# Keys and values of a cross attention layer by one level of Strassen's scheme, on a kernel in float32

## The chip, the core and the metric

The kernel runs on one core of a Trainium2 chip. TensorE multiplies matrices into PSUM; VectorE (DVE), ScalarE (ACT) and GpSimd (POOL) work elementwise on SBUF, the first two also on PSUM; SyncE (SP) issues most of the DMAs, in order. Each engine works through its own queue of instructions in program order and waits on semaphores for the others. The metric is the device time of one execution in microseconds, as a median over runs.

## The reference, cut to what matters

A perceiver of two layers over x (16 batches of 64 queries, 512 channels) and a context (16 batches of 1601 rows, 512 channels). Everything is float32. The change is in the second layer, L1, and at its border to the first:

```python
x = x + L0_xattn(...); x = x + L0_attn(...); x = x + L0_ffn(...)      # experts, top 2 of 8 and 2 shared
# L1 cross attention: D = 512, H = 16 heads of HD = 32
q = split_heads(layernorm(x) @ Wq + bq)          # 64 queries a batch
k = split_heads(ctx @ Wk + bk)                   # 1601 keys a batch
v = split_heads(ctx @ Wv + bv)
scores = where(mask, -1e15, einsum('bhqd,bhkd->bhqk', q, k) / sqrt(32))
o = einsum('bhqk,bhkd->bhqd', softmax(scores), v)
x = x + o @ Wo + bo
# per row of x: differential attention over 32 half heads of 16, then a feed forward 512-2048-512 (relu)
x = x + L1_attn(layernorm(x), ...)
# feed forward with ternary weights and quantised activations, with a width 3 convolution along the queries
x = x + L1_ffn(layernorm(x), ...)
```

K and V of the context, 16 x 1601 x 512 x 512 multiplications each, are the largest matrix products of the layer.

## The kernel before, in words

x is held as eight tiles `g.x[t]` of 128 rows (two batches each), which stay in SBUF from the first line to the last. L0 ends in `l0_ffn`: experts write their results to a DRAM buffer `worked`, and a last loop gathers them by GpSimd's indirect DMAs and adds them to the tiles of x (L666). The weights Wk and Wv are loaded there already (`g.wk`, `g.wv`). Tiles come from pools; a tile with a tag and n buffers waits for the last reader of the n-th one before it. The PSUM tags are `mm` (4 banks), `tp` (2) and `acc` (2).

`l1_layer` is a loop over 16 batches b, and in each over four groups f of four heads (128 channels). The keys of a batch are cut into four tiles `KC` of 384, 384, 384 and 449.

- `load_ctx(b)` loads the transposed context, channels on the partitions, as four tiles `ctxT` and `ctxT_last`; it is called when f = 2 of the batch before is done.
- `project_k(b, f, n)` makes K transposed for one group f and one key tile: four accumulating matmuls whose moving tensor is the context tile (384 or 449 columns); ScalarE copies it to `kT` with the bias. In step (b, f) it is called for the group that comes next, for all four tiles.
- `project_v(b, half, n)` makes V with keys on the partitions, for 256 channels: per 128 keys four matmuls whose stationary tensor is the context and whose moving tensor is Wv, 256 columns; ScalarE copies it to `v`. Called in the even steps for f // 2.
- `scores` makes the scores of two banks at a time, and VectorE's `copy_predicated` (L832) writes the unmasked ones into `p`, which GpSimd has filled with -1e15 (L1192). Then per `p` a maximum on VectorE (L1202) and an exponential on ScalarE (L1203).
- `transpose_keys` (L182, L185) transposes the p of the step before, and `attend` (L842) multiplies it with v. So the softmax of a step is used one step later.
- `finish` scales the output by the reciprocal row sums: rs8 is transposed (L855), inverted on VectorE, and spread over the channels by eight pairs of matmuls with the constant `spread` (L861). For the second batch of a tile Wo, and the residual into `g.x[t]`, follow.
- `queries(t)` makes the queries of a tile of x, with Wq loaded in halves.
- `later(t)` is the rest of the layer for a tile that has its cross attention: a generator with a `yield` after each piece. Its large VectorE work is `products` (L895 multiplies, L896 sums, 16 rounds for q by k and 8 for the weights by v). It ends in `last(t)`, the ternary feed forward.

The order of the work is written out by hand: after the scores of a step, four rounds n = 0 to 3 follow, each with `project_k`, in round 0 also `attend`, in even steps `project_v`, and then `run(behind, quota)`, that lets so many pieces of `later` of the tile before run. `later(t)` begins at f = 0 of an even batch and runs out at the end of the odd one. In the first two batches `behind` is `ternary_weights`, which prepares the ternary weights. Before the loop, batch 0's context is loaded, K and V of its first groups are made, and the queries of tile 0.

`load_cols` and `load_rows` load weights in pieces of 512 KB from a pool of six buffers; `load_row` loads a bias row, spread over the partitions, once for the whole layer (x1_bo, a1_bo, a1_b2).

Of the kernel before, what the change touches and what calls it, by code (L numbers as in the profile page):

```python
# [2 lines left out]

# [7 lines left out]
F32 = mybir.dt.float32  # L11
# [426 lines left out]
def l0_ffn(g, d):  # L438
# [8 lines left out]
    with ExitStack() as es:  # L447
# [210 lines left out]
        for t in range(NT):  # L658
            for k in range(2):
# [8 lines left out]
                )  # L668


KC = [(0, 384), (384, 384), (768, 384), (1152, 449)]


def l1_layer(g, d, out):
# [5 lines left out]
    with ExitStack() as es:  # L680
# [3 lines left out]
        cpool = pool("x1_c", 3)  # L684
        kpool = pool("x1_k", 6)
        vpool = pool("x1_v", 15)
# [3 lines left out]
        spool = pool("x1_s", 1)  # L690
        apool = pool("a1_s", 1)
        prod = pool("a1_prod", 1)
        wpool = pool("l1_w", 6)

        x1bo = load_row(g, one, "x1_bo")
        a1bo, b2 = load_row(g, one, "a1_bo"), load_row(g, one, "a1_b2")
# [6 lines left out]
        spread = one.tile([NP, 2, NC, P], F32, tag="spread", name="spread")  # L703
        nc.gpsimd.memset(spread, 0.0)
        for j in range(2):
            for pl in range(2):
                nc.gpsimd.memset(spread[:, j, :, ds((2 * pl + j) * HDX, HDX)], 1.0)
            nc.gpsimd.affine_select(
                out=spread[:, j], in_=spread[:, j], compare_op=ALU.is_equal, fill=0.0,
                base=0, pattern=[[-2, NC], [-1, 2], [0, 2 * HDX]], channel_multiplier=1,  # L710
            )
# [37 lines left out]
        ctxs, kTs, vs = {}, {}, {}  # L749

        def load_ctx(b):
            for n, (k0, w) in enumerate(KC):
                tag = "ctxT" if n < 3 else "ctxT_last"
                t = cpool.tile([P, NC, w], F32, tag=tag, name=tag, bufs=None if n < 3 else 1)
                nc.sync.dma_start(
                    out=t, in_=g.ctx_T[b, :, k0 : k0 + w].rearrange("(c p) k -> p c k", p=P)
                )
                ctxs[b, n] = t

        def project_k(b, f, n):  # L760

            w = KC[n][1]
            ps = mm(g)
            mm_k(g, ps[:, :w], lambda c: wk[:, c, ts(f, P)], lambda c: ctxs[b, n][:, c, :])
            tag = "kT" if n < 3 else "kT_last"
            kT = kpool.tile([P, w], F32, tag=tag, name=tag, bufs=None if n < 3 else 2)
            nc.scalar.activation(kT, ps[:, :w], AF.Identity, bias=col(g, "x1_bk", f))  # L767
            kTs[b, f, n] = kT

        def project_v(b, half, n):  # L770

            k0, w = KC[n]
            for k in range((w + P - 1) // P):
                kw = min(P, w - k * P)
                ps = mm(g)
                mm_k(
                    g, ps[:kw, :256],
                    lambda c: ctxs[b, n][:, c, ds(k * P, kw)],
                    lambda c: wv[:, c, ts(half, 256)],
                )  # L780
                v = vpool.tile([P, 256], F32, tag="v", name="v")
                nc.scalar.copy(v[:kw], ps[:kw, :256])  # L782
                vs[b, half, k0 // P + k] = v[:kw]

        def queries(t):

            u = apool.tile([P, D], F32, tag="u2", name="u")
            ln_apply(g, u, g.x[t], ln_stats(g, small, [g.x[t]]), 0)
            yield
            uT = apool.tile([P, NC, P], F32, tag="u2T", name="uT")  # L790
            nc.scalar.copy(uT, transpose4(g, u))
            yield
# [5 lines left out]
            qT = spool.tile([P, NC, P], F32, tag="qT", name="qT", bufs=2)  # L798
# [37 lines left out]
        def attend(b, f, pTs, po):  # L836
# [3 lines left out]
            for k in reversed(range(len(KT))):  # L840
                for r in reversed(range(4)):
                    nc.tensor.matmul(  # L842
                        po[ts(r, HDX), ts(f, S)],
                        lhsT=vs[b, f // 2, k][:, ts(4 * (f % 2) + r, HDX)],
# [6 lines left out]
        def finish(b, po, rs8):  # L851
            t, hb = divmod(b, 2)

            pt = mm(g, tag="tp")
            nc.tensor.transpose(pt[:NP, :P], rs8, g.ident)  # L855
            rsT = small.tile([NP, P], F32, tag="rsT", name="rsT")
            nc.vector.reciprocal(rsT, pt[:NP, :P])
            pr = mm(g, tag="tp")
            for f in range(NC):
# [503 lines left out]
```

## Time and profile before

| what | value |
|---|---|
| median of 3 runs | 3542.52 us (3540.64 to 3544.93) |
| the profiled execution, by the device | 3548.19 us |
| its span, first to last instruction | 3546.4 us |
| mean granted clock of TensorE | 0.968 |
| L146 MATMUL, K, 384 columns | 1536, busy 555.2 us |
| L146 MATMUL, V, 256 columns, context tiles 0 to 2 | 2304, busy 523.7 us |
| L146 MATMUL, V, tile 3 | 1024, busy 226.2 us |
| L146 MATMUL, K, 449 columns | 512, busy 206.4 us |
| L832 COPY_PREDICATED, L1202 maximum, DVE | 270.4 and 226.5 us |
| L895 and L896, products, DVE | 156.5 and 155.8 us |
| L185 and L782, copies of pT and v, ACT | 230.7 and 152.4 us |
| L1192 memset of p, POOL | 185.7 us |

A group of instructions has a mean duration, but the records of TensorE overlap: the time between starts of neighbours is what a matmul costs in a stream. A float32 matmul leaves two records and two weight loads. The idle time of an engine before a group is put down to what released it last. The first 790 us are L0; the loop over batches starts at about 843 us, and two batches take between 321 and 326 us. The chain of work that ended last is followed on the page only through part of the span, TensorE 9% and DVE 6%, so the windows and the timeline carry more.

### The profile page before, as it was taken

The numbers are of one execution on the slowest core, as the hardware profiler recorded it, in microseconds if no ns is written. First come the engines' busy times: TensorE is split into PE (matmuls) and PEld (weight loads), VectorE is DVE, ScalarE is ACT, GpSimd is POOL, SyncE is SP. The second block draws the span as 40 slices with busy tenths as digits, with TensorE's granted clock in tenths as the row PEclk, the third lists the DMA queues.
The fourth block names the chain that finished last, engine by engine and source line by source line (L and its number), as shares of the span: only waits on it lengthen the run. The fifth ranks groups of instructions, "written<-read, shape, count | busy, mean of one in ns | idle before, by whom it ended". The sixth has DMA issues, their size and how long they took to land. (4 is left out here: it accounts for less than half of the span.)

```text
span 3546.4 us, 49781 instructions
## 1 busy us (share of the span) xinstructions
PE 3275.7 (92%) x21128; PEld 2194.3 (62%) x21128; DVE 1652.8 (47%) x2632; ACT 1140.0 (32%) x2220; POOL 377.5 (11%) x340
## 2 busy tenths in 40 slices
PE   6999999998999999999999999999999999999815
PEld 2444445685677666766767666667667676666514
DVE  2121223116525825653493458256534934581573
ACT  1111021112333434334333434343343334343402
POOL 0000003332101100010001001000100010010000
PEclk9999999999999999999999999999999999999957
DMA  9988413875611133113222321331132123213113
GB/s 361 313 288 304 140 36 107 283 254 174 196 50 50 40 107 103 57 43 123 95 65 74 111 75 40 107 103 57 44 124 97 61 74 111 75 41 107 63 36 122
DMA packets 267374, 418.03 MB, mean 118 GB/s; under 512 B 20736, under 2 KB 164224, under 8 KB 267152
## 3 DMA queue, kind: packets, MB, share of 16 engines
q1 hardware_dynamic: 254656, 370.28, 31.7%
q0 software_dynamic: 12496, 44.57, 3.6%
q8 instruction: 166, 2.72, 0.3%
q14 instruction: 56, 0.46, 0.0%
HBM read 392.26 MB, written 22.54 MB: 117 GB/s over the span
## 5 line engine op out<-in xcount | busy, mean ns | idle before, releaser
L146 PE MATMUL ps_mm<-ctxT,wkv 128*128 128x384 f32 x1536 | 555.2, 492 | 2.0 <-DVE p L832 0.4
L146 PE MATMUL ps_mm<-wkv,ctxT 128*128 128x256 f32 x2304 | 523.7, 380 | 0.0
L146 PEld LDWEIGHTS ps_mm<-wkv,ctxT 128*128 128x128 f32 x2304 | 434.0, 190 | 80.1
L832 DVE COPY_PREDICATED p<-mk,ps_mm 128x384 f32<-128x384 uint8 (+1 forms) x512 | 270.4, 596 | 332.8 <-PE ps_mm L824 332.7
L1192 POOL MEMSET p<- 128x1601 f32 x128 | 185.7, 1453 | 1822.9 <-PE ps_tp L182 1819.1
L146 PEld LDWEIGHTS ps_mm<-ctxT,wkv 128*128 128x128 f32 x1536 | 272.6, 191 | 134.0 <-DVE p L832 7.8
L185 ACT COPY pT<-ps_tp 128x512 f32<-128x512 f32 x504 | 230.7, 504 | 356.2 <-PE ps_tp L182 356.1
L782 ACT COPY v<-ps_mm 128x256 f32<-128x256 f32 (+1 forms) x416 | 152.4, 370 | 417.4 <-PE ps_mm L146 416.7
L182 PEld LDWEIGHTS ps_tp<-ident,p 128*128 128x128 f32 (+1 forms) x1768 | 199.9, 143 | 135.0 <-issue 56.7
L182 PE MATMUL ps_tp<-ident,p 128*128 128x128 f32 (+1 forms) x1768 | 255.4, 282 | 6.4 <-ACT pT L87 3.0
L1202 DVE TENSOR_REDUCE negm<-p 128x1 f32<-128x1601 f32 x128 | 226.5, 1810 | 1.2
L146 PE MATMUL ps_mm<-wkv,ctxT_last 128*128 128x256 f32 (+1 forms) x1024 | 226.2, 379 | 0.0
L895 DVE TENSOR_TENSOR prod<-qkv 128x1024 f32<-128x1024 f32 x128 | 156.5, 1223 | 138.4 <-ACT qkv L927 134.8
L1203 ACT ACTIVATE p<-p,negm 128x1601 f32<-128x1601 f32 x128 | 208.0, 1627 | 15.1 <-DVE negm L1202 14.6
L146 PEld LDWEIGHTS ps_mm<-wkv,ctxT_last 128*128 128x128 f32 (+1 forms) x1024 | 181.1, 177 | 48.6 <-issue 12.1
L146 PE MATMUL ps_mm<-ctxT_last,wkv 128*128 128x449 f32 x512 | 206.4, 540 | 0.0
L824 PE MATMUL ps_mm<-kT,qbd 64*128 64x384 f32 x768 | 197.7, 531 | 8.1 <-DVE qbd L813 8.0
L767 ACT ACTIVATE kT<-ps_mm,cols 128x384 f32<-128x384 f32 x192 | 109.3, 579 | 188.7 <-PE ps_mm L146 188.7
L146 PEld LDWEIGHTS ps_mm<-hT,w 128*128 128x128 f32 x1024 | 132.2, 194 | 56.2 <-ACT hid L1011 40.6
L896 DVE TENSOR_REDUCE att<-prod 128x64 f32<-128x1024 f32 x128 | 155.8, 1217 | 3.7
L146 PEld LDWEIGHTS ps_mm<-ctxT_last,wkv 128*128 128x128 f32 x512 | 95.6, 190 | 81.1 <-issue 73.5
L146 PE MATMUL ps_mm<-hT,w 128*128 128x128 f32 x1024 | 142.6, 283 | 2.4 <-ACT hid L1011 1.0
(291 smaller groups left out, 3872.3 us busy)
## 6 DMA issues: line engine op xcount, KB each, us to landing
ctxT<-in_ctx_T_dram SPq DMA_DIRECT2D x48, 1024.0 KB, 10.4
ck<-in_ctx_dram SPq DMA_DIRECT2D x48, 1024.0 KB, 7.3
ctxT<-in_ctx_T_dram SPq DMA_DIRECT2D x48, 768.0 KB, 4.4
w<-in_W1T_dram SPq DMA_DIRECT2D x64, 512.0 KB, 4.6
w<-in_W2T_dram SPq DMA_DIRECT2D x64, 512.0 KB, 3.7
wt<-tern SPq DMA_DIRECT2D x64, 512.0 KB, 4.2
ctxT_last<-in_ctx_T_dram SPq DMA_DIRECT2D x16, 898.0 KB, 4.8
w<-in_x_Wq_dram SPq DMA_DIRECT2D x16, 512.0 KB, 3.8
```

What stands on the lines that cost most here:

```text
L146: g.nc.tensor.matmul(out, lhsT=lhs(c), rhs=rhs(c), start=(c == 0), stop=(c == n - 1))
L182: g.nc.tensor.transpose(pt[:kw, j, :], p[:, k0 + j * P : k0 + j * P + kw], g.ident)
L185: (out_of or (lambda o, i: evac(g, o, i)))(pT[:kw, :blocks, :], pt[:kw, :blocks, :])
L767: nc.scalar.activation(kT, ps[:, :w], AF.Identity, bias=col(g, "x1_bk", f))
L782: nc.scalar.copy(v[:kw], ps[:kw, :256])
L824: nc.tensor.matmul(bank[:, : KC[n][1]], lhsT=qbd[ts(j, 2 * HDX), f].rearrange("p j s -> p (j s)"), rhs=kTs[b, f, n][ts(j, 2 * HDX), :], st ...
L832: nc.vector.copy_predicated(ps_[j][:, k0 : k0 + w], mk[:, k0 : k0 + w], bank[:, :w])
L895: nc.vector.tensor_tensor(pr, qv.unsqueeze(2).to_broadcast([P, CH, 32, 16]), kv, ALU.mult)
L896: nc.vector.tensor_reduce(out[:, ts(i, CH * 32)], pr.rearrange("p i j d -> p (i j) d"), AX.X, ALU.add)
L1192: nc.gpsimd.memset(p, -1e15)
L1202: nc.vector.tensor_reduce(negm, p, AX.X, ALU.max, negate=True)
L1203: nc.scalar.activation(p, p, AF.Exp, bias=negm, accum_out=sums[:, 2 * f + j : 2 * f + j + 1])
```

## The change

K and V of the context are made by one level of Strassen's scheme in Winograd's form: a product of two matrices cut into 2 x 2 blocks is made of seven products of blocks, with sums before and after.

- The context tile is cut into two halves of channels and, for each of two halves of 768 keys (m), into two blocks of 384 keys. The last 65 keys (`rest`) are multiplied in the plain way. The weights are cut into halves of input channels and, for each 256 output channels, two groups of 128.
- `weight_sums` makes the sums of the weights once, on VectorE. `sum_ctx(b)` makes the differences of a batch's context on GpSimd: per half of the keys four of 128x768, and one for the rest.
- `seven` makes the seven products, each in one `mm` bank of 384 columns (two matmuls of 384 for K, three times two of 128 for V), and puts them together: five copies on ScalarE, two adds with a PSUM operand on VectorE, five adds of 384 on GpSimd.
- `project_k(b, h, m)` makes two groups f at once. It is called in the odd steps: at f = 1 for the second two groups of the batch, at f = 3 for the first two of the next, after that batch's `sum_ctx`. `project_v(b, h, m)` is called in the even steps.
- The pieces of `later` per round are 2, 3, 2, 3 in every step (at f = 0 of an even batch 1, 1, 2, 3), where they were 1 in odd steps, 3 at f = 0 and 4 at f = 2.
- x goes through DRAM: `l0_ffn` stores each tile to `between`, the tiles in SBUF are given up at the end of L0, and `queries` and `finish` load them again.
- The three bias rows are loaded per tile into one buffer (`row_of`), the weights' pool has four buffers instead of six, qT one instead of two.
- `finish` inverts rs8 on VectorE, spreads it with `side` into `wide` (128x512) and folds it by four matmuls with `fold`; the transpose goes.

```diff
+            nc.sync.dma_start(out=g.between[ts(t, P), :], in_=g.x[t])
...
-KC = [(0, 384), (384, 384), (768, 384), (1152, 449)]
+KB = 384
+K4 = 4 * KB
+KR = S2 - K4
+KC = [(n * KB, KB + (KR if n == 3 else 0)) for n in range(4)]
...
-        cpool = pool("x1_c", 3)
+        spool = pool("x1_s", 1)
+        cpool = pool("x1_c", 2)
+        wsum = pool("x1_w", 1)
         kpool = pool("x1_k", 6)
-        vpool = pool("x1_v", 15)
+        tpool = pool("x1_t", 1)
+        vpool = pool("x1_v", 4)
...
-        wpool = pool("l1_w", 6)
+        wpool = pool("l1_w", 4)
+        def row_of(name):
+            r = apool.tile([P, D], F32, tag="row", name="row")
+            i = _ROWS[name]
+            nc.sync.dma_start(out=r, in_=g.rows[i : i + 1, :].to_broadcast([P, D]))
+            return r
...
+        def weight_sums(w, name):
...
+            for c in range(2):
+                nc.vector.tensor_tensor(s3[:, c], a11[:, c], a21[:, c], ALU.subtract)
+                nc.vector.tensor_tensor(a21[:, c], a21[:, c], a22[:, c], ALU.add)
+                nc.vector.tensor_tensor(s2[:, c], a21[:, c], a11[:, c], ALU.subtract)
+                nc.vector.tensor_tensor(s4[:, c], a12[:, c], s2[:, c], ALU.subtract)
+            return {"11": a11, "12": a12, "22": a22, "s1": a21, "s2": s2, "s3": s3, "s4": s4}
...
         def load_ctx(b):
+            src = g.ctx_T[b].rearrange("(i c p) k -> p i c k", i=2, p=P)
+            for m in range(2):
+                x = {}
+                for i in range(2):
+                    for n in range(2):
+                        t = cpool.tile([P, 2, KB], F32, tag=f"x{i}{n}", name="ctx")
+                        nc.sync.dma_start(out=t, in_=src[:, i, :, ts(2 * m + n, KB)])
+                        x[f"{i + 1}{n + 1}"] = t
+                xs[b, m] = x
...
+        def sum_ctx(b):
+
+            for m in range(2):
...
+                nc.gpsimd.tensor_tensor(t1, x["12"], x["11"], ALU.subtract)
+                nc.gpsimd.tensor_tensor(t2, x["22"], t1, ALU.subtract)
+                nc.gpsimd.tensor_tensor(t4, x["21"], t2, ALU.subtract)
+                nc.gpsimd.tensor_tensor(x["12"], x["22"], x["12"], ALU.subtract)
+                x.update(t1=t1, t2=t2, t3=x.pop("12"), t4=t4)
...
+            add = lambda o, a, b: nc.gpsimd.tensor_tensor(o, a, b, ALU.add)
+            p1, u2, u3, p5 = new("p1"), new("u2"), new("u3"), new("p5")
+            put(p1, times("11", "11"), None)
+            nc.vector.tensor_tensor(u2, times("s2", "t2"), p1, ALU.add)
+            put(c11, times("12", "21"), above)
+            add(c11, c11, p1)
+            p7 = times("s3", "t3")
+            if below is None:
+                nc.vector.tensor_tensor(u3, p7, u2, ALU.add)
+            else:
+                nc.vector.scalar_tensor_tensor(u3, p7, below, u2, ALU.add, ALU.add)
+            put(p5, times("s1", "t1"), None)
+            add(c22, u3, p5)
+            add(p5, p5, u2)
+            put(c12, times("s4", "22"), above)
+            add(c12, c12, p5)
+            put(c21, times("22", "t4"), None)
+            add(c21, c21, u3)
...
         def queries(t):
...
+            nc.sync.dma_start(out=u, in_=g.between[ts(t, P), :])
+            ln_apply(g, u, u, ln_stats(g, small, [u]), 0)
...
-            pt = mm(g, tag="tp")
-            nc.tensor.transpose(pt[:NP, :P], rs8, g.ident)
-            rsT = small.tile([NP, P], F32, tag="rsT", name="rsT")
-            nc.vector.reciprocal(rsT, pt[:NP, :P])
+            r8 = small.tile([P, NP], F32, tag="r8", name="r8")
+            nc.vector.reciprocal(r8, rs8)
...
             for f in range(NC):
-                for j in range(2):
-                    nc.tensor.matmul(
-                        pr[:, ts(f, S)], lhsT=spread[:, j, f, :], rhs=rsT[:, ts(j, S)],
-                        start=(j == 0), stop=(j == 1),
-                    )
+                nc.tensor.matmul(
+                    pr[:, ts(f, S)],
+                    lhsT=wide[:, ts(f, 2)].rearrange("p h j d -> p (h j d)"), rhs=fold,
+                    start=True, stop=True,
+                )
...
         load_ctx(0)
-        for n in range(len(KC)):
-            project_k(0, 0, n)
-            project_v(0, 0, n)
+        sum_ctx(0)
+        for project in (project_k, project_v):
+            for m in range(2):
+                project(0, 0, m)
         run(queries(0))
...
+                if f % 2 == 0:
+                    work = [partial(project_v, b, f // 2, m) for m in range(2)] if b + f > 0 else []
+                else:
+                    bk, h = (b, 1) if f == 1 else (b + 1, 0)
+                    if f == 3 and bk < B:
+                        sum_ctx(bk)
+                    work = [partial(project_k, bk, h, m) for m in range(2)] if bk < B else []
+                for n in range(4):
+                    if n % 2 == 0 and work:
+                        work.pop(0)()
+                    run(behind, 1 if b % 2 + f == 0 and n < 2 else 2 + n % 2)
                     if n == 3:
                         run(asked, 1)
```

## The prediction

> **What bounds the kernel now.** I read the busy line first, then the layer's inside, since an average over two layers says little.
>
> ```profile
> PE 3275.7 (92%) x21128; PEld 2194.3 (62%) x21128; DVE 1652.8 (47%) x2632; ACT 1140.0 (32%) x2220; POOL 377.5 (11%) x340
> ```
>
> By it TensorE bounds the kernel and VectorE has half its time free. The table by windows corrects that for one pair of batches: an even batch's steps f = 0, 1, 2, 3 (one row each), then the whole odd batch. Columns after the length: busy us and instructions per engine, clock, DMA.
>
> ```profile
> core 0: us, PE busy (x) PEld busy (x) DVE busy (x) ACT busy (x) POOL busy (x), PEclk, DMA share, GB/s
> 2052.96:2112.20 59.24, 58.52 (x372) 45.49 (x371) 27.26 (x38) 19.10 (x40) 4.15 (x3) 1.00 0.29 89
> 2112.20:2132.84 20.64, 19.50 (x176) 11.65 (x175) 20.37 (x21) 9.78 (x16) 2.87 (x2) 1.00 0.16 49
> 2132.84:2176.53 43.69, 42.41 (x283) 31.46 (x282) 40.60 (x41) 15.30 (x30) 4.08 (x4) 1.00 0.18 55
> 2176.53:2202.27 25.74, 23.18 (x179) 14.15 (x179) 21.00 (x30) 10.99 (x19) 2.87 (x2) 0.87 0.15 45
> 2202.27:2379.00 176.73, 171.86 (x1247) 121.99 (x1246) 67.20 (x133) 73.92 (x147) 15.57 (x11) 1.00 0.30 94
> ```
>
> In steps 1 to 3 of the even batch (90.07 us together) VectorE is busy for 81.97 us and TensorE for 85.1: both are nearly full. Only f = 0 and the odd batch (DVE 38%) are TensorE's alone. So a cut of matmuls pays in about 236 us of every 326, and VectorE work added to the other 90 is paid in full.
>
> The pace of matmuls is read from starts in the timeline of TensorE, not from mean durations, which include the overlapped pipeline (each float32 matmul is two records):
>
> ```profile
> 2024.84 3.73 PE L146 MATMUL ps_mm<-uT,w 128*128 128x128 f32 x32
> 2028.51 1.76 PE L824 MATMUL ps_mm<-kT,qbd 64*128 64x384 f32 x8
> ...
> 2067.84 1.99 PE L861 MATMUL ps_tp<-rsT,spread 8*128 8x64 f32 x16
> 2069.77 1.99 PE L146 MATMUL ps_mm<-wkv,ctxT 128*128 128x256 f32 x8
> ...
> 2075.05 2.74 PE L146 MATMUL ps_mm<-ctxT,wkv 128*128 128x384 f32 x8
> 2077.63 5.34 PE L146 MATMUL ps_mm<-wkv,ctxT 128*128 128x256 f32 x24
> 2082.81 2.74 PE L146 MATMUL ps_mm<-ctxT,wkv 128*128 128x384 f32 x8
> ```
>
> Per record: 384 columns (2077.63 - 2075.05)/8 = 0.3225 us; 256 columns 5.18/24 = 0.2158; 128 columns, each with its own weights, 3.67/32 = 0.1147; the spread matmuls 1.93/16 = 0.12. The 449 column records that start at 2098.73 are 0.3775 apart.
>
> **K and V, TensorE.** A unit is two heads' groups f (256 channels) over all 1601 keys; 16 batches have 32 of each. K before: 2 x (24 x 0.3225 + 8 x 0.3775) = 21.5 us. After: 2 halves x 7 products x 2 matmuls = 56 records x 0.3225 = 18.1, and 16 records of 65 columns at the 128 column pace (the nearest, an upper end) = 1.8; 19.9, so -1.6. V before: 13 key tiles x 8 records x 0.2158 = 22.4. After: 2 x 7 x 3 key tiles x 2 matmuls = 168 records of 128 columns x 0.1147 = 19.3, the last 65 keys 1.8; 21.1, so -1.3. With 31 units each outside the start: -50 and -40. The finish part: 16 spread records and a transpose become 8 records: -1.1 x 16 = -17. TensorE's sum: **-107 us**, 3%, not the eighth that "seven of eight" suggests, since the last 65 keys take short matmuls of their own and V's matmuls, of half the columns, keep a slightly worse pace per column.
>
> V rests on the pace of 128 columns. The Trainium skill, "TensorE: Matmul & The Clock Gate", section "Back-to-back issue gap", speaks against it: a stream of weight load and matmul pairs at N = 128 keeps about 81 ns instead of the isolated 56, 1.45 times. Scaled so, a record costs about 0.156 (estimate from that page), V becomes 28.7 us a unit and the change loses 7.6 x 31 = 235 us more. The trace has this very stream, 32 such pairs at 0.1147, half of 0.2158; I take the row.
>
> **Evacuation: new work on VectorE, ScalarE and GpSimd.** Each group of seven products (four a batch for K, four for V) is copied out by five ScalarE instructions of 384 (a 512 copy takes 0.585, a 256 copy 0.37; so 0.48), two VectorE adds (256 from PSUM 0.425, 512 0.691; so 0.56) and five GpSimd adds. GpSimd's adds of 512 take 1.27 and of 256 0.62 (the multiply of att by am): 2.5 ns an element, so 0.97 for 384. A batch gets 40 such adds, 39 us, and eight context differences of 768 at 1.9, 15 us: GpSimd goes from about 15 to 69 us of 160, and from 377 to some 1240 us in all. It fits, if nobody waits for it.
>
> The order of VectorE's and TensorE's instructions in the built kernels, priced by these rows, gives per step. Even batch, TensorE: before 58.2, 18.3, 41.3, 18.8; after 45.0, 27.4, 29.2, 27.9. VectorE: before 28.3, 21.2, 42.3, 16.4; after 19.2, 30.8, 31.6, 31.0. The even quotas of 2, 3, 2, 3 pieces in each step spread the pieces that were bunched. But steps 1 to 3 now ask 93.4 us of VectorE (before 79.9 by the same sum: 6.7 for twelve adds, the rest pieces pulled out of f = 0), against 84.5 of TensorE. **VectorE becomes the bound of this stretch.** Odd batch, TensorE: 167.5 before, 160.6 after; VectorE 87 at most, no bound.
>
> Three things come on top of 93.4. Idle gaps: before, 8.1 of 90.07; I take 6. The wait for GpSimd: the trace shows the two holding each other where both read:
>
> ```profile
> 1264.12 1.27 POOL L1001 TENSOR_TENSOR u<-u,row_a_b 128x512 f32<-128x512 f32 x1 [3.76 <-DVE ln_rstd L99]
> 1264.27 1.40 DVE L117 TENSOR_SCALAR u<-xt,ln_mv,ln_rstd 128x512 f32<-128x512 f32 x1
> ```
>
> The line before it in the timeline is the same VectorE operation in 0.55: it waited till GpSimd ended. The VectorE work here is mostly another form, prod<-qkv with two operands in SBUF, 1.22 us. No row shows one beside a reading add. The Trainium skill, "SBUF — State Buffer", section "Who interferes with whom", has it contend, exclusively[...]. Below: 0, no gain possible. Above: some 20 such instructions, each behind a whole add, 19 us. GpSimd reads in about 45% of the time (48 of 107 us), a hit waits half an add, 4.4 us; adds come in pairs, so I take 8. Sum 93.4 + 6 + 8 = 107.
>
> **Sum for the pairs.** Even batch before 149.3 (59.24 + 90.07); after 45.0 + 1.3 idle + 107.2 = 153.5: +4.2. Odd batch 160.6 + 9.2 (its excess over the sum now: 176.7 - 167.5) = 169.8: -6.9. Seven pairs: +29 and -48. Batches 0 and 1, with no later layer behind them, have TensorE sums of 219.5 and 208: about -10. The tail, with r8, wide and a reload of x: +2.
>
> **The start.** Now K and V of batch 0 run while layer 0 still combines its experts:
>
> ```profile
> 816.21 7.07 PE L146 MATMUL ps_mm<-wkv,ctxT_last 128*128 128x256 f32 x32
> 827.28 0.77 PE L126 MATMUL ps_tp<-ident,u 128*128 128x128 f32 x4 [4.01 <-issue]
> 828.77 6.54 PE L146 MATMUL ps_mm<-uT,w 128*128 128x128 f32 x32 [0.72 <-ACT uT L791]
> 843.27 2.93 PE L824 MATMUL ps_mm<-kT,qbd 64*128 64x384 f32 x8 [7.96 <-DVE qbd L813]
> ```
>
> The 33 us from 789 to 823 are free. After, the context tiles sit where x was, so their loads wait for x's stores to DRAM, and on SP's queue they stand behind eight stores, the load of u (which waits for all of them) and Wq. The last combination ends at 821.2; a 256 KB store lands in 5.3; so loads start at 827, tiles land by 831 to 832 (4.4 us for 768 KB), the second product waits for GpSimd's t2 and t3, until some 838. Then K 20, V 21 and the queries: scores at about 884 instead of 843.3. **+41**, between +33 (loads slip ahead of the last stores) and +48 (V waits for the sums of the second half as well).
>
> **Costed at nothing.** Memsets of p stand behind the adds on GpSimd; they are early by a step, and if not, the scores wait a 1.45 us memset. The reloads of x (256 KB) and of three rows per tile stand on SP between weight loads; the row buffer is single, and a row waits for its last reader with the next weights behind it. Two pieces, some 5 us, lie between, which covers a landing of 4.6; uncovered it is 4.6 x 8 = 37. Four weight buffers for six: a 512 KB load lands in 3.7 to 4.6, a half takes 16 records, 3.6 us, so two ahead suffice. The four temporaries are single: the next group's copy of p1 waits for one add, over long before.
>
> **Total.** -10 + 41 + 29 - 48 + 2 = +14 on the profiled 3548.2, so 3562; the median shown lies 5.7 lower, so **3557 us**.
>
> **Rivals.** *Faster, for want of the wait.* If VectorE's products pass GpSimd's adds freely and its gaps fill, the stretch takes 98 instead of 107, a pair saves 9 x 7 = 63: 3557 - 63 = **3494**. For it: no row shows prod waiting, and the pieces are spread well. Against: the L117 pair above. *GpSimd becomes the bound.* Step f = 3 queues nine context differences (16 us) ahead of K's ten adds, together 30 us of the 28 to 31 that the step has; the scores of the next step need kT whole. If the last adds come late by 5 us in each of 15 batches, +75: **3632**. It decides when the tiles of x land later than the middle of f = 3's softmax; against it, three pieces of work stand between K's last product and the scores. *Nothing to tell*: start and loss cancel the gain, 3536 to 3550. *V at the page's pace*: 3790; the row excludes it nearly.
>
> **Chances.** A measurement of this kernel tells some 0.2%, 7 us, from no change. Forecast 0.50 (own range 3536 to 3590, of which about a tenth lies within 7 us of 3542.5), the faster rival 0.28, GpSimd 0.16, cancelled 0.05, V's pace 0.01. Faster 0.31, same 0.11, slower 0.58. Range: the lock's ends (0 to 19 for 8: -56, +77) and the start's (-8, +7) reach both rivals: 3480 to 3632.
>
> **What would show it.** First scores of the layer near 884, TensorE idle from 790 to 831. V's records of 128 columns 0.115 apart. Windows of the even batch's steps 1 to 3: 105 to 110 us with VectorE above 90% (right), or TensorE above 95% in 98 us (the first rival). Rows of prod well above 1.22 us. Releasers of idle TensorE: DVE u2, u3 or p for me, POOL kT or ctx sums for the second. The period of a pair: 326 to 323. I am wrong if the start costs under 30 us, or if the even batch gets shorter than 149.

## The result, and the profile after

The changed kernel takes 3729.48 us (median of 4 runs, 3724.13 to 3737.66), the one before 3543.72 us (median of 4, 3540.64 to 3546.29). The ratio is 1.0527, 95% interval 1.0505 to 1.0549: **186 us slower**, where +14 was forecast. The profiled execution has a span of 3729.6 us and a mean granted clock of 0.931 (before 0.968).

The busy line of the page:

```profile
PE 3256.8 (87%) x23785; PEld 2295.5 (62%) x23800; DVE 1899.2 (51%) x2921; ACT 1185.4 (32%) x2283; POOL 1349.8 (36%) x1120
```

TensorE is busy for about as long as before, in a longer span; GpSimd went from 377.5 to 1349.8 us. The table by windows of the changed kernel, for the same pair of batches as before: the even batch's steps 0 to 3, then the whole odd batch.

```profile
core 0: us, PE busy (x) PEld busy (x) DVE busy (x) ACT busy (x) POOL busy (x), PEclk, DMA share, GB/s
2162.14:2207.74 45.60, 45.06 (x411) 40.38 (x410) 18.60 (x32) 17.66 (x36) 14.74 (x14) 1.00 0.24 73
2207.74:2236.83 29.09, 29.06 (x216) 17.97 (x215) 28.82 (x30) 13.36 (x23) 12.61 (x9) 1.00 0.13 42
2236.83:2272.20 35.37, 33.35 (x331) 28.50 (x330) 32.38 (x33) 12.16 (x24) 21.12 (x15) 0.90 0.32 90
2272.20:2316.12 43.92, 33.43 (x219) 20.76 (x218) 33.73 (x36) 13.47 (x24) 29.17 (x23) 0.84 0.04 9
2316.12:2514.59 198.47, 174.64 (x1412) 132.36 (x1413) 92.73 (x167) 78.41 (x153) 74.25 (x63) 0.94 0.32 99
```

The even batch takes 154.0 us for 149.3, as forecast (153.5). The odd batch takes 198.5 for 176.7, where 169.8 was forecast. Two things stand out: the clock (0.90, 0.84 and 0.94 in step 2, step 3 and the odd batch, where it was 1.00, 0.87 and 1.00) and, in step 3, no engine that is nearly full: TensorE 33.4, VectorE 33.7, GpSimd 29.2 of 43.9.

Over the six pairs in the middle, summed from the records of the trace, a pair went from 325.1 to 349.6 us:

| us in a pair | before | after | change |
|---|---|---|---|
| TensorE idle | 10.5 | 35.5 | +25.0 |
| lost at half clock (half of TensorE's busy time in stretches with a granted clock of 0.5) | 2.2 | 16.2 | +14.0 |
| the rest, TensorE's work at full clock | 312.4 | 297.9 | -14.5 |

The saving is there. It is given back nearly twice over in idle time, and once more in clock.

**Where step 3 waits.** The timeline of the changed kernel, all engines, with lines left out:

```profile
2279.31 2.17 PE L961 MATMUL ps_mm<-kT,qbd 64*128 64x449 f32 x6
2279.58 0.58 DVE L969 COPY_PREDICATED p<-mk,ps_mm 128x384 f32<-128x384 uint8 x1
...
2281.49 1.80 POOL L804 TENSOR_TENSOR ctxsum<-ctx,ctxsum 128x768 f32<-128x768 f32 x1
2283.25 1.80 POOL L806 TENSOR_TENSOR ctx<-ctx 128x768 f32<-128x768 f32 x1
2285.01 1.80 POOL L805 TENSOR_TENSOR ctxsum<-ctx,ctxsum 128x768 f32<-128x768 f32 x1
2286.77 0.62 POOL L1099 TENSOR_TENSOR att<-att,am 128x256 f32<-128x256 f32 x1
...
2287.72 0.62 POOL L1099 TENSOR_TENSOR att<-att,am 128x256 f32<-128x256 f32 x1
2288.37 0.43 DVE L1104 TENSOR_TENSOR att<-att 128x256 f32<-128x256 f32 x1 [8.22 <-POOL att L1099]
2288.72 0.58 DVE L969 COPY_PREDICATED p<-mk,ps_mm 128x384 f32<-128x384 uint8 x1
...
2289.35 1.00 PE L961 MATMUL ps_mm<-kT,qbd 64*128 64x384 f32 x1 [7.87 <-DVE p L969]
```

Read it from the end. TensorE idles 7.87 us for a bank that a masked copy (L969) must empty. The copy stands on VectorE behind L1104, which idles 8.22 us for the scaling of att on GpSimd (L1099), two operations of 0.62 us that belong to the tile of the two batches before. They stand behind the differences of the next batch's context. Nobody in this chain needs a difference: three queues, each in order, pass the delay on.

**The clock after a stall.** TensorE's timeline a little later, and the windows of the two stretches (columns as above):

```profile
2324.69 2.93 PE L901 MATMUL ps_mm<-wkv,ctx 128*128 128x128 f32 x12
...
2329.10 1.50 PE L901 MATMUL ps_mm<-wkv,ctx 128*128 128x128 f32 x12
```

```profile
2321.30:2328.10 6.80, 6.58 (x22) 4.91 (x23) 6.42 (x15) 1.02 (x2) 0.00 (x0) 0.50 0.00 0
2328.10:2334.50 6.40, 6.40 (x59) 6.40 (x59) 4.77 (x9) 5.65 (x7) 0.00 (x0) 1.00 0.00 0
```

The same twelve records take 2.93 us at a clock of 0.50 and 1.50 at 1.00. The stretch at half clock began right after idle times of 2.31 and 0.51 us. The Trainium skill, "TensorE: Matmul & The Clock Gate", section "Why this matters for your kernels", warns of idle gaps above about 3 us; here, in even step 3 and odd step 0 of the pair, gaps of 2.3 to 7.9 us came with 3.4 to 10.2 us at half clock. Shorter ones did too: in step 2 of the same batch (clock 0.90 in the table) two gaps of 1.44 and 0.56 us stand right before 6.8 us at half clock, from 2242.8 on.

```profile
2240.88 0.99 PE L961 MATMUL ps_mm<-kT,qbd 64*128 64x449 f32 x2 [1.44 <-POOL kT L829]
2242.43 1.52 PE L961 MATMUL ps_mm<-kT,qbd 64*128 64x449 f32 x2 [0.56 <-DVE p L969]
```

The length of a gap does not settle it: in e4 below a gap of 3.08 us (it ends at 2677.3) was followed by full clock. The prediction had no term for the clock.

### The profile page after: what moved, and what is told of

It reads as the page before. It is cut to its first block, busy times and chain, and to the rows that moved or that the text cites. A ratio compares the mean times of both kernels' runs of the same rounds, so it can differ in the third digit from the quotient of the medians.

```text
span 3729.6 us, 57282 instructions
## 1 busy us (share of the span) xinstructions
PE 3256.8 (87%) x23785; PEld 2295.5 (62%) x23800; DVE 1899.2 (51%) x2921; ACT 1185.4 (32%) x2283; POOL 1349.8 (36%) x1120
## 3 DMA queue, kind: packets, MB, share of 16 engines
q8 instruction: 188, 3.08, 0.3%
## 5 line engine op out<-in xcount | busy, mean ns | idle before, releaser
L961 PE MATMUL ps_mm<-kT,qbd 64*128 64x384 f32 (+1 forms) x1024 | 310.2, 596 | 113.1 <-DVE p L969 81.1
L969 DVE COPY_PREDICATED p<-mk,ps_mm 128x384 f32<-128x384 uint8 (+1 forms) x512 | 279.4, 594 | 211.9 <-PE ps_mm L961 211.2
L865 PE MATMUL ps_mm<-ctx,wkv 128*128 128x384 f32 x512 | 204.7, 514 | 54.0 <-DMA ctx<-in_ctx_T_dram 38.4
L829 POOL TENSOR_TENSOR v<-v,p 128x384 f32<-128x384 f32 x128 | 146.6, 1145 | 274.5 <-ACT v L825 271.3
L901 PE MATMUL ps_mm<-wkv,ctx 128*128 128x128 f32 x1536 | 217.1, 289 | 0.7
L901 PE MATMUL ps_mm<-wsum,ctx 128*128 128x128 f32 x1536 | 199.2, 278 | 17.4 <-DVE u L832 17.4
L901 PEld LDWEIGHTS ps_mm<-wkv,ctx 128*128 128x128 f32 x1536 | 199.4, 204 | 9.8 <-DVE o L1118 7.5
L901 PE MATMUL ps_mm<-wkv,ctxsum 128*128 128x128 f32 x1536 | 197.4, 277 | 0.0
L901 PEld LDWEIGHTS ps_mm<-wsum,ctx 128*128 128x128 f32 x1536 | 185.0, 194 | 19.4 <-DVE u L832 18.7
L865 PE MATMUL ps_mm<-ctx,wsum 128*128 128x384 f32 x512 | 187.6, 489 | 5.6 <-DVE u L832 5.6
L865 PE MATMUL ps_mm<-ctxsum,wkv 128*128 128x384 f32 x512 | 189.4, 493 | 0.0
```

What stands on the lines that cost most here:

```text
L829: add = lambda o, a, b: nc.gpsimd.tensor_tensor(o, a, b, ALU.add)
L865: nc.tensor.matmul(bank, lhsT=aks[i][:, c, h, :], rhs=x[j][:, c, :], start=c == 0, stop=c == 1,)
L901: nc.tensor.matmul(bank[:, ts(k, P)], lhsT=x[j][:, c, ts(k, P)], rhs=avs[i][:, c, h, :], start=c == 0, stop=c == 1,)
L961: nc.tensor.matmul(bank[:, : KC[n][1]], lhsT=qbd[ts(j, 2 * HDX), f].rearrange("p j s -> p (j s)"), rhs=kTs[b, f, n][ts(j, 2 * HDX), :], st ...
L969: nc.vector.copy_predicated(ps_[j][:, k0 : k0 + w], mk[:, k0 : k0 + w], bank[:, :w])
```

## The experiments

Steps are the mean of the six middle pairs, from the first score matmul of a step to that of the next; the last column is us in a pair, counted as above. The kernels that leave the adds or the differences out, or their results unused (e7, e10, e12 to e15, e18), do not make the right K and V: they tell times, and are no alternatives.

| kernel | median us | even 0 | 1 | 2 | 3 | odd 0 | 1 | 2 | 3 | half clock lost |
|---|---|---|---|---|---|---|---|---|---|---|
| before | 3543.7 | 59.3 | 20.6 | 43.7 | 24.5 | 65.2 | 35.4 | 51.8 | 24.5 | 2.2 |
| after | 3729.5 | 45.6 | 29.1 | 35.3 | 44.1 | 73.2 | 47.4 | 34.8 | 40.2 | 16.2 |
| e1_att_on_dve | 3697.2 | 45.6 | 29.1 | 35.0 | 38.9 | 74.0 | 47.4 | 35.3 | 40.5 | 17.2 |
| e5_quota_before | 3662.3 | 45.6 | 29.0 | 31.2 | 45.1 | 56.2 | 47.0 | 40.6 | 45.1 | 12.3 |
| e7_no_adds | 3593.6 | 45.7 | 28.8 | 32.6 | 35.0 | 71.3 | 47.0 | 36.8 | 34.2 | 8.4 |
| e12_no_pool_quota | 3459.1 | 45.6 | 28.8 | 29.8 | 32.3 | 55.8 | 47.0 | 35.6 | 36.7 | 2.8 |
| e14_no_sums_quota | 3497.4 | 45.6 | 29.0 | 31.4 | 33.3 | 57.9 | 47.0 | 34.5 | 36.6 | 3.6 |
| e15_no_pool | 3547.0 | 45.7 | 28.8 | 32.8 | 30.8 | 72.0 | 47.1 | 33.4 | 34.0 | 6.8 |
| e16_sums_on_dve | 3625.0 | 45.6 | 29.1 | 32.2 | 39.5 | 66.5 | 47.0 | 34.7 | 38.9 | 12.6 |
| e18_sums_unused | 3663.4 | 45.6 | 29.0 | 32.5 | 43.9 | 56.1 | 47.0 | 38.5 | 47.2 | 11.1 |

**The single late links first.** The theory after the result was that a few late links make the idle time: the scaling of att, and pieces of `later` in rounds that have no matmuls of K or V beside them.

```diff
-                nc.gpsimd.tensor_tensor(
+                nc.vector.tensor_tensor(
                     att[:, hs, hs], att[:, hs, hs],
```

> The changed kernel with the scaling of att by am (L1099) on VectorE instead of GpSimd. Theory (late links): in step 3 of each even batch that scaling stands on GpSimd behind the context differences, VectorE waits 8.2 us for it with the masked copies of the scores behind it, and TensorE idles 6.9 us; then it runs at half clock. Without it the step falls from 44 to 31-35 us, a pair from 349.7 to 337-341, in all 3640-3670 us. Rival (VectorE's amount of work, or its waits for GpSimd's port, sets that step): two more instructions on VectorE, the step stays at 43-45, in all 3725-3740 us.

3697.2 us, ratio to before 1.0428 (1.0411 to 1.0446), 32 us less than the change. TensorE's idle time in step 3 fell from 9.6 to 3.2 us, but the step fell only by 5.2 us: 1.2 us more are lost at half clock, and VectorE (busy 37.6 us of 38.9) is right behind. That is about half of what was expected.

```diff
             p7 = times("s3", "t3")
...
+            yield
             put(p5, times("s1", "t1"), None)
...
-                    if n % 2 == 0 and work:
-                        work.pop(0)()
+                    if work:
+                        run(work[n // 2], 1 if n % 2 == 0 else None)
```

> The changed kernel with each group of seven products given out in two portions of four and three, one for each of the four rounds of a step, so that every round has matmuls of K or V between the pieces of the layer's rest; nothing else. Theory (late links): the chains of small links in the odd batch (6.3 us before the transposes of z, 1.5 to 2.7 us each at dg, qT, u and W2T) find cover and the half clock after them goes: odd batch from 195.6 to 172-182 us, in all 3610-3660 us. Rival (the amount of work, or GpSimd): 3715-3740 us.

3727.3 us, ratio 1.0518 (1.0501 to 1.0536): nothing, as the rival has it. The wait before the transposes of z (6.3 us a pair) became two, of 2.0 us before the transposes of o and 2.6 before those of z, and the step did not get shorter (74.4 us for 73.2): a pair has 3.1 us less of idle time and loses 2.5 us more at half clock (18.7 for 16.2). Cover by matmuls was not what was missing.

> Both edits, the scaling of att on VectorE and the portions of four and three products. Theory: the gains add, a pair takes 318-330 us instead of 349.7, in all 3510-3600 us, with the half clock under 15 us a pair instead of 42.7. Rival: 3700 us or more.

Both edits: 3687.2 us, ratio 1.0404 (1.0387 to 1.0421), stretches at half clock still 39.8 us a pair. This is far from the theory's 3510-3600; the theory of single links fell here.

**The quotas.** Their line alone, in the kernel before (e4), and its reverse in the changed one (e5):

```diff
-                    run(behind, 1 if f % 2 == 1 or b % 2 + f == 0 and n < 2 else 3 + f // 2)
+                    run(behind, 1 if b % 2 + f == 0 and n < 2 else 2 + n % 2)
```

> The kernel before with the quotas of pieces of the changed one (2, 3, 2, 3 in every step) and nothing else of the change. Theory: with matmuls of K in each of the four rounds the chains stay covered, the quotas by themselves cost little: 3530-3580 us. Rival (the quotas are what costs, by where the pieces fall): 3640 us or more.

3607.8 us, ratio 1.0174 (1.0144 to 1.0203): 63 us lost, between the ranges of theory and rival. Even step 2 went from 43.7 to 49.2 us, odd step 0 from 65.2 to 76.4. Of the 9.5 us that a pair grew, 5.4 were lost at half clock and only 1.4 are idle time.

> The changed kernel with the quotas of pieces of the one before (1 in odd steps, 3 at f = 0, 4 at f = 2) and nothing else. Theory: the even spreading costs the changed kernel what it cost the one before (63 us there), so 3650-3685 us. Rival: the quotas suit the new placing of K and V (VectorE's 42 us of step 2 stay unspread), 3725-3760 us.

3662.3 us, ratio 1.0333 (1.0316 to 1.0350): 67 us back, mostly in odd step 0 (73.2 to 56.2), against 11 lost in the odd steps 2 and 3. The even spreading, which the prediction took for a good, costs about 65 us in either kernel.

> The changed kernel with the quotas of before, the portions of four and three products, and the scaling of att on VectorE. Theory: the three gains add: 3605-3645 us, a pair in 332-337 us, half clock down to 15-30 us a pair. Rival (the sum of work on VectorE and its waits for GpSimd bound the whole, wherever the pieces stand): 3680 us or more.

With the two edits of e3 on top: 3660.5 us, ratio 1.0330 (1.0313 to 1.0347), the same as e5 and between the two ranges. The gains don't add.

**GpSimd's part.** The adds left out:

```diff
             put(c11, times("12", "21"), above)
-            add(c11, c11, p1)
...
-                nc.vector.tensor_tensor(u3, p7, u2, ALU.add)
+                nc.vector.tensor_tensor(c22, p7, u2, ALU.add)
...
-            add(c22, u3, p5)
-            add(p5, p5, u2)
...
```

> The changed kernel without the five adds of each group of seven products on GpSimd (left out: c11 + p1, u3 + p5, p5 + u2, c12 + p5, c21 + u3; u3 goes to c22 itself), so K and V are incomplete; copies, VectorE's adds and all matmuls stay. Theory (GpSimd costs through the late scaling of att, the last adds before the scores, and the slowed prod, together about 60 us): 3655-3690 us. Rival A (GpSimd stands behind nearly all of the loss): 3540-3600 us. Rival B (it costs nothing): 3720-3735 us.

3593.6 us, ratio 1.0139 (1.0122 to 1.0156): 136 of the 186 us, more than twice what the theory gave GpSimd, and at the upper edge of rival A's range. Most of the loss goes with GpSimd's adds, by their time, their port or the links they add.

In e10 each add is three memsets of its output:

```diff
-            add = lambda o, a, b: nc.gpsimd.tensor_tensor(o, a, b, ALU.add)
+            add = lambda o, a, b: [nc.gpsimd.memset(o, 1.0) for _ in range(3)]
```

> The changed kernel with each of the five adds on GpSimd replaced by three memsets of its output (about the same time on GpSimd, nothing read), so K and V are constants. It splits the 136 us of the kernel without the adds. If the cost is that VectorE and GpSimd hold each other's port when both read: prod back near 1.22 us, and 3610-3660 us. If it is the time on GpSimd's queue: prod back to 1.22 us too, but 3700-3735 us. If neither matters but the order in which results come: 3594 us, as without adds.

3673.2 us, ratio 1.0361 (1.0346 to 1.0377), between the first two: of the 136 us some 56 are there only if GpSimd reads, 80 also if it only writes (roughly: a memset waits for fewer inputs than the add, and the memsets take 802 us in all, the adds 725). The rows of the products, of the weights with v in the changed kernel, then of the same in e10, then of q with k in e10 (minimum, median, maximum in ns):

```profile
L1040 DVE TENSOR_TENSOR prod<-att,qkv x64: 1201/1225/2047, 1240.7 to 3624.6; 128x1024 f32<-128x1024 f32 x64
```

```profile
L1040 DVE TENSOR_TENSOR prod<-att,qkv x64: 1207/1218/1226, 1232.2 to 3571.0; 128x1024 f32<-128x1024 f32 x64
L1040 DVE TENSOR_TENSOR prod<-qkv x128: 1206/1224/2645, 1151.2 to 3540.4; 128x1024 f32<-128x1024 f32 x128
```

Of the first, the longest took 2047 ns beside two adds; of the second, the longest of which have memsets beside them, none took over 1226. The third reach 2645 ns, and the longest of them overlap the context differences, which e10 still makes and which read. The Trainium skill, "SBUF — State Buffer", section "Who interferes with whom", which the prediction weighed, has a VectorE instruction with two inputs in SBUF contend with a GpSimd instruction that reads and not with one that only writes; that is what is seen.

Adds moved instead of left out (e9): c11, c12 and c21 by VectorE straight from PSUM (with the quotas of before, and att on VectorE):

```diff
-            put(c12, times("s4", "22"), above)
-            add(c12, c12, p5)
+            join(c12, times("s4", "22"), above, p5)
```

> The changed kernel with the quotas of before and the scaling of att on VectorE, and of the five adds of a group three (c11, c12, c21) made by VectorE straight from PSUM, in place of a copy on ScalarE and an add on GpSimd each. Theory (the adds cost by standing on GpSimd, as queue and as port): three fifths of the 136 us that leaving them out gained come back, less some 13 us a batch of VectorE work where it is the bound, so 3590-3640 us, against 3662 with the quotas alone. Rival (VectorE's amount decides): 3680-3740 us.

3688.8 us, ratio 1.0416 (1.0400 to 1.0432): 27 us worse than e5. GpSimd fell from 1346 to 915 us, VectorE rose to 2046, and odd step 0 went from 56.2 to 65.2. The rival holds.

Then the adds and the differences both left out, at the quotas of before (e12):

```diff
-                nc.gpsimd.tensor_tensor(t1, x["12"], x["11"], ALU.subtract)
...
-                x.update(t1=t1, t2=t2, t3=x.pop("12"), t4=t4)
+                x.update(t1=x["11"], t2=x["22"], t3=x.pop("12"), t4=x["21"])
```

> The changed kernel with the quotas of before, without the five adds of a group and without the differences of the context (the products read the context's blocks themselves), so K and V are incomplete; all matmuls, copies, and VectorE's adds stay. Theory (TensorE's saving of 107 us is there, and GpSimd's work with the quotas hides it): before, less 80 to 107, and 27 for the start: 3460-3500 us. Rival (the groups' copies and links between engines cost as well): 3520-3560 us.

3459.1 us, ratio 0.9764 (0.9749 to 0.9779). The prediction's own arithmetic for TensorE and the measured start (below) give 3543.7 - 107 + 27 = 3464, or 3458 with the first scores of e12 itself (864.6, so +21). All the matmuls, ScalarE's copies and VectorE's adds are in this kernel, and so are x's way through DRAM, the smaller pools and the new `finish`: the change does not lose by these. Its pair of batches, in the same windows as above:

```profile
core 0: us, PE busy (x) PEld busy (x) DVE busy (x) ACT busy (x) POOL busy (x), PEclk, DMA share, GB/s
...
2095.18:2125.02 29.84, 29.75 (x332) 26.87 (x331) 29.53 (x32) 12.19 (x24) 2.87 (x2) 1.00 0.31 93
2125.02:2157.33 32.31, 31.09 (x220) 19.32 (x219) 30.80 (x38) 13.06 (x24) 4.11 (x4) 0.95 0.09 25
2157.33:2332.67 175.34, 169.23 (x1414) 127.19 (x1414) 78.40 (x164) 76.63 (x153) 15.30 (x11) 0.99 0.31 99
```

Step 2 has TensorE and VectorE both full, step 3 takes 32.3 us instead of 43.9 (45.0 in e5), and VectorE is busy for 78 us of the odd batch, where e5, with the same quotas and the same VectorE instructions, has 93:

```profile
2236.15:2281.15 45.00, 33.37 (x220) 20.67 (x219) 35.52 (x38) 13.37 (x24) 31.31 (x25) 0.85 0.04 9
2281.15:2470.96 189.81, 176.77 (x1414) 131.09 (x1413) 92.82 (x165) 76.37 (x153) 72.99 (x62) 0.95 0.29 92
```

**Adds or differences.** At the quotas of before, one at a time (e13, e14), and both away at the quotas of the change (e15):

> The changed kernel with the quotas of before and without the five adds of a group; the differences of the context stay on GpSimd (K and V incomplete). It splits the 203 us between 3662 (quotas of before alone) and 3459 (adds and differences left out too). If the adds are the cost by themselves: 3465-3490 us. If adds and differences cost by standing in one queue, each about half: 3540-3580 us. If the differences are the cost: 3630 us or more.

3535.9 us, ratio 0.9975 (0.9965 to 0.9984): -126 from e5, nearest to the case of one shared queue.

> The changed kernel with the quotas of before and without the differences of the context (the products read the blocks themselves); the five adds of a group stay on GpSimd (K and V incomplete). With only 15 us a batch less on GpSimd against 39 for the adds: if cost goes with time on GpSimd, 3600-3615 us; if the block of eight differences ahead of other work is what holds the scores, 3520-3570 us; if the adds alone are the cost, 3650 us or more.

3497.4 us, ratio 0.9877 (0.9859 to 0.9895): -165 from e5, below all three ranges. Fifteen us of GpSimd a batch cost more than the thirty-nine of the adds; and with the differences away the adds cost only 3497.4 - 3459.1 = 38. By steps (e5 less e14) the differences cost 11.8 us in even step 3, 6.1 and 8.5 in the odd steps 2 and 3, and nothing in the others.

> The changed kernel with its own quotas, without the adds and the differences (K and V incomplete). If the quotas cost what they cost the kernel before and the changed one, some 65 us: 3515-3530 us. If their cost came from GpSimd's queue and port in the stretches they fill: 3459-3480 us.

3547.0 us, ratio 1.0010 (1.0002 to 1.0019), 88 above e12 and above both ranges. The quotas cost by themselves, without these works of GpSimd: a pair takes 324.6 us for 311.7, 9.4 of it more idle time and 4.0 more lost at half clock. Odd step 0 takes 72.0 instead of 55.8 us, in part because work of other steps moved there, with 5.1 us a pair of idle time before the transposes of z and 10.8 us of stretches at half clock.

What the differences do is seen in the timeline of e5, in the convolution of an odd batch:

```profile
2407.39 1.86 POOL L804 TENSOR_TENSOR ctxsum<-ctx,ctxsum 128x768 f32<-128x768 f32 x1
2407.49 3.72 DVE L1279 SCALAR_TENSOR_TENSOR y<-hs,cols,y 128x126 f32<-128x126 f32 x2
2409.20 1.86 POOL L806 TENSOR_TENSOR ctx<-ctx 128x768 f32<-128x768 f32 x1
2411.02 1.86 POOL L805 TENSOR_TENSOR ctxsum<-ctx,ctxsum 128x768 f32<-128x768 f32 x1
2411.13 2.15 DVE L1275 SCALAR_TENSOR_TENSOR y<-hs,cols,y 128x126 f32<-128x126 f32 x2
2413.20 0.60 DVE L1279 SCALAR_TENSOR_TENSOR y<-hs,cols,y 128x126 f32<-128x126 f32 x2
...
2413.88 1.28 ACT L1285 ACT_TABLE_LOAD   x1 [6.35 <-DVE y L1279]
...
2423.67 1.87 PE L147 MATMUL ps_mm<-uT,wt 128*128 128x128 bf16 x16 [3.20 <-ACT v L825]
```

Two convolution steps (L1279) take 0.60 us when GpSimd is idle, the last line of VectorE, and 3.72 us beside the differences: each waits for one whole difference. The mean of these instructions, 256 with those of L1275, is 344 ns before, 341 in e12, 470 in the changed kernel and 634 in e5. Behind them wait ScalarE's sT (6.35 us idle before its table load), behind that ScalarE's copies of V, and TensorE for their banks (3.20 us).

Moved to VectorE, every sum kept (e16, the first pair of lines), and then four pieces moved from even step 3 to odd step 1 (e17, the last pair, against e16):

```diff
-                nc.gpsimd.tensor_tensor(t1, x["12"], x["11"], ALU.subtract)
+                nc.vector.tensor_tensor(t1, x["12"], x["11"], ALU.subtract)
...
-                    run(behind, 1 if f % 2 == 1 or b % 2 + f == 0 and n < 2 else 3 + f // 2)
+                    run(behind, (((1, 3)[n // 2], 1, 4, 0), (3, 2, 4, 1))[b % 2][f])
```

> The changed kernel, whole, with the quotas of before and the context differences on VectorE instead of GpSimd. Without the differences and with the adds 3497 us were measured. Eight differences of 768 cost VectorE some 0.95 us each, 7.5 us a batch. Theory (the block on GpSimd's queue is what cost 165 us, VectorE has room for them in the odd batch's step 3, not in the even one's): 3525-3555 us. Rival (the time the differences take counts, wherever they stand): 3590 us or more.

3625.0 us, ratio 1.0230 (1.0212 to 1.0248): 37 less than e5, 128 above e14. The rival: where they stand changes little. They are nearly as much in the way on VectorE, where a difference took 0.94 to 1.76 us (L803, L804) and 43.0 us in all were spent idle in front of them for the landing of the context. On GpSimd, in e5, that wait was 7.7 us, so this kernel has a link more, and how much of the 128 us is the link's is not shown.

> As the last, and the four pieces of the even batch's step 3 moved to the odd batch's step 1 (quotas 1 1 3 3, 1, 4, 0 and 3, 2, 4, 1), where VectorE has 13.5 us of work in 47. Theory: the even step 3 falls from some 39 to 31-34 us and the odd step 1 grows by the pieces' matmuls alone: 3490-3535 us, below the kernel before. Rival (the pieces that shift bring new late links): 3540-3580 us.

3634.3 us, ratio 1.0257 (1.0238 to 1.0276). Above both ranges: even step 3 stayed at 39.7, though it has four pieces less, and odd step 1 grew by the 20 us that odd step 0 lost (67.1 for 47.0, 46.1 for 66.5).

Last, the wait for the differences' results taken away, and their time kept: GpSimd makes them, the products read the blocks.

```diff
-                x.update(t1=t1, t2=t2, t3=x.pop("12"), t4=t4)
+                x.update(t1=x["11"], t2=x["22"], t3=x.pop("12"), t4=x["21"])
```

> The changed kernel with the quotas of before; GpSimd makes the differences of the context as ever, but the products read the blocks themselves, so that no matmul waits for a difference (K and V incomplete). Against 3662 us with the differences used and 3497 us without them. If their cost is the time they take on GpSimd's queue, with other work behind them: 3635-3665 us. If their cost is that the first products of K wait for them: 3495-3530 us.

3663.4 us, ratio 1.0335 (1.0318 to 1.0352), against 3662.3 with the differences used. **The wait for a difference's result costs nothing.** The differences cost by the time they take, in GpSimd's queue (step 3 above) and at the port (the convolution); what each of the two is worth for them was not measured apart.

**Parts of the change alone.** V in the plain way in the kernel of e6, K by sevens (e8):

```diff
+                    for c in range(4):
+                        nc.tensor.matmul(
+                            ps[:, :256], lhsT=tiles[c // 2][:, c % 2, ts(j, P)],
+                            rhs=wv[:, c, ts(h, 256)], start=c == 0, stop=c == 3,
+                        )
```

> As the kernel with the quotas of before, the portions and the scaling on VectorE, but V is made in the plain way (four matmuls of 256 columns per 128 keys, one copy on ScalarE), and K by the seven products. Theory (what a group of seven couples costs more than its matmuls save): 20 to 60 us below that kernel. Rival (TensorE's work sets the end): V's saving is given up, 40 us above that kernel.

3645.6 us, ratio 1.0293 (1.0276 to 1.0310), 15 below e6, short of the expected 20 to 60. In that kernel V's sevens cost some 15 us more than they save.

And the new `finish` alone in the kernel before (e11, its hunk of the change's diff):

> The kernel before with the new finish alone (inverse on VectorE, wide, four matmuls with fold; no transpose, no spread). By the sum of the prediction 1.1 us less of TensorE in each of 16 batches, at a place where TensorE is the bound: 3524-3532 us. Rival (wide, 0.7 us on VectorE, and its link to the matmuls cost what is saved): 3540-3550 us.

3527.4 us, ratio 0.9955 (0.9942 to 0.9969), 15 us below before, in the expected range (17 by the sum). **This is the one kernel here, complete in its computation, that beats both.**

## Why the prediction was wrong

**TensorE's sum: right.** 107 us were worked out. The middle pairs show 14.5 us each (13.8 by the sum), and e12 lands within 5 us of it. V's records of 128 columns:

```profile
844.21 1.50 PE L901 MATMUL ps_mm<-wsum,ctxsum 128*128 128x128 f32 x12
845.55 1.50 PE L901 MATMUL ps_mm<-wkv,ctx 128*128 128x128 f32 x12
```

1.34 us for 12, 0.112 each; the row of before (0.1147) decided rightly against the pace estimated from the Trainium skill's page (0.156).

**The start: right in kind, too large.** TensorE idles 38.4 us for the context as foreseen, but the first scores come at 870.3 instead of 884, +27 for +41. That is under the 30 us which the prediction had named as a sign of being wrong. The term that failed is "The last combination ends at 821.2": without K and V beside it L0's combination issued its last add at 809.3 instead of 820.4, and the context was there at 817.1, where 831 to 832 was worked out.

```profile
817.12 2.90 PE L865 MATMUL ps_mm<-ctx,wkv 128*128 128x384 f32 x4 [38.41 <-DMA ctx<-in_ctx_T_dram]
...
870.30 5.88 PE L961 MATMUL ps_mm<-kT,qbd 64*128 64x384 f32 x24 [1.53 <-DVE qbd L950]
```

**The even stretch: right sum, partly for another reason.** 107 us forecast, 108.4 measured. In step 1 VectorE is full (28.8 of 29.1), as said, though TensorE's records fill it too. Step 3 is not VectorE's: it waits for GpSimd through the scaling of att, which the sum had not seen. VectorE is busy for 94.9 of the 108.4 us, 88%, where the prediction named over 90% as the sign that it is right. That the sum came out is luck in this part.

**The odd batch: here it failed.** "Odd batch 160.6 + 9.2 (its excess over the sum now)" carries the excess of before over to a batch with nearly five times GpSimd's work (74.3 us for 15.6), and takes VectorE's margin ("87 at most, no bound") for safety. Measured 195.5 in the mean: 23 us of idle time and 8 lost at half clock, where the odd batch of the kernel before has 5 and 0. Twenty-six us a pair too few, in seven pairs, are 180, as much as the whole miss of 172.

**The step behind it** is "It fits, if nobody waits for it". GpSimd's share was measured against the length of a batch, 69 of 160 us. What counts is who stands behind it. The prediction even took this scaling of att (256 in 0.62 us) for GpSimd's pace, and did not ask who waits for it: VectorE idled 7.8 us for it over the middle of the kernel before, 57.5 us in the changed one. The port was counted for prod alone, at 8 us a pair. Prod lost 31 us in the eight tiles, some 4 a pair. The small convolution steps, which were not listed though they are 88 us of VectorE, lost 32 us (470 for 344 ns), and 74 in e5. GpSimd came out larger too: its adds took 1.03 to 1.28 us in the mean where 0.97 was counted, and it was busy for 1350 us where some 1240 were. The rival of GpSimd named the engine rightly but as a wait for kT: TensorE waited for kT 10.1 us in all (the line is below), and e18 excludes the differences' results. Where it had +75, GpSimd's adds and differences cost 3662 - 3459 = 203 at the quotas of before.

```profile
PE ps_mm L961 <- POOL kT L829: 10.1, 7, 1.4
```

**The quotas** were counted as a gain ("spread the pieces that were bunched"); e4 and e5 show a loss of 63 and 67 us. What makes it stays open: in the kernel before it is half clock more than idle time (e4), in e15 it is more idle time than clock (9.4 and 4.0 us a pair), and e2 took the wait for z apart without any effect.

**The clock** was missing: 14 of the 39 us given back in a pair. It came beside more idle time here, but not in proportion (e4: 5.4 us lost for 1.4 us of idle time), and the runs show no rule that would have given its size.

Summed in the order in which they were taken away: 67 for the quotas, 165 for the differences, 38 for the adds, 27 for the start, against 107 saved: +190, measured +186. The first three are differences of successive kernels, so they add up by construction; what the sum tests is e12 alone, worked out 80 us below before and measured 85. The order matters: adds first, they count 126 and the differences 77, since one delays the other.

## What to carry to other kernels

A busy share of an idle engine is no measure of what new work there costs. List what stands behind each new instruction in that engine's queue, and what shares its port, the shortest operations too. Where TensorE sets the time, read the granted clock after each idle gap, since a slow stretch can follow, and compare a saving of 3% on one engine with all the links that it adds between the others.

## What the runs showed that was not expected

A VectorE operation of 0.34 us took up to 1.90 us (the maximum of L1275) beside a GpSimd subtraction of 1.86 us. Long operations lose as much, so short ones lose more in proportion: prod, 1.22 us, took up to 2.84 beside such subtractions in e7. Idle gaps of 1.44 and 0.56 us, one right after the other, came before 6.8 us at half clock. And GpSimd, busy for 32% of the time in e14, could not take 15 us more in each batch without 165 us in the total: 11 us for each of 15 batches, whether its results were used (e5) or not (e18).
